# Sixteen experts on one core: the last six token tiles behind a branch on a count made on chip

## The chip, the cores and the metric

The kernel runs on one core of one Trainium2 chip. The metric is device time in microseconds of that core for one execution of the whole kernel. The kernel before takes 2091.18 us, the median of three runs (2089.25 to 2093.39).

## The reference, cut to what matters

Two layers of "graph attention, then feed-forward" over 3327 nodes with 256 features. The change lies in the first layer's feed-forward part, a mixture of 16 experts with the two best experts per token:

```python
logits = jnp.einsum('bsd,de->bse', x, gate_w) + gate_b
probs = jax.nn.softmax(logits, axis=-1)
top_probs, top_idx = jax.lax.top_k(probs, 2)
top_probs = top_probs / jnp.sum(top_probs, axis=-1, keepdims=True)
dispatch = jnp.sum(jax.nn.one_hot(top_idx, n_experts, dtype=x.dtype) * top_probs[..., None], axis=-2)
h1 = jnp.einsum('bsd,edh->bseh', x, w1)
h2 = jnp.einsum('bsd,edh->bseh', x, w2)
hidden = jax.nn.silu(h1) * h2
expert_out = jnp.einsum('bseh,eho->bseo', hidden, w3)
return jnp.einsum('bseo,bse->bso', expert_out, dispatch)
```

Here x is the layer-normalised node feature (256), the hidden width is 512, and only the two chosen experts of a token have a nonzero weight. Ahead of it stands a graph attention with two heads and a residual add; behind it a graph attention with one head, and a recurrence of 30 steps (tanh, silu, layer norm, a 256 x 256 product). All of that is the same in both kernels.

## The kernel before, in words

The nodes lie in 26 tiles of 128 rows. During the first graph attention every finished group of tiles is routed: normalised rows are written to a DRAM table (`table_x`), the gate picks two experts per token, and POOL's indirect DMAs write each token's number and weight into one list per expert (`lists`, line 551).

Only tokens that chose an expert are computed for it. Each expert's list is cut into tiles of 128 tokens, the last one partly empty. Whatever the routing, 2 x 3327 pairs over 16 experts fill at most `SLOTS` = (6654 - 16) // 128 + 16 = 67 tiles, and the kernel before works off 67 tiles always. Lines 605 to 675 make on chip, from the experts' counts (`cnt`: column 0 the tokens, column 2 the tiles, columns 3 and 4 the first tile and the end), the tables by tile: the expert (`table`, row 0), whether its weights differ from those three tiles earlier (`table`, row 1), which rows to gather (`which`), where to put results (`to`) and their weights. Tiles past the last expert's carry no tokens: `mine` is zero for them, their expert is 0, and their results go to spare rows of `given` that nothing reads.

The stage at lines 724 to 761 is a loop over tiles written out, on all engines at once. For each tile: POOL gathers 128 rows by indirect DMA four tiles ahead (line 685); TensorE transposes them (line 711) and ScalarE copies the result; TensorE multiplies with w1 (`pa`) and w2 (`pb`, both line 720); ScalarE takes silu of `pa` (line 741), VectorE multiplies with `pb` into `hidT` (line 744). One tile later TensorE multiplies `hidT` with w3 (`po`, line 751), VectorE scales by the token's weight (`y`, line 753), and POOL scatters `y` into the DRAM tensor `given` (line 754). Weights rotate through `SETS` = 3 sets of buffers; SyncE loads a set two tiles ahead (`weights`, lines 692 to 705), three DMAs of 512 KB, each carried out only when the register `new` is not zero. The first three sets are loaded unconditionally. SyncE reads expert and `new` from `table` into registers by one table load per tile.

After the stage, `add_results` (lines 776 to 785) reads `given` back by DMAs on SyncE (`th`, `z`, line 782), and VectorE or POOL adds them into x; then layer 1 begins with its projection. A scheduler puts the instructions in order within each engine and inserts the semaphore waits. The first reload of `given` waits for all scatters.

Of the kernel before, what the change touches and what calls it, by code (L numbers as in the profile page):

```python
# [10 lines left out]
F32 = mybir.dt.float32  # L11
I32 = mybir.dt.int32
BF16 = mybir.dt.bfloat16
FP8 = mybir.dt.float8e4
AF = mybir.ActivationFunctionType
ALU = mybir.AluOpType
# [3 lines left out]
P = 128  # L20
# [9 lines left out]
def gat_moe_gat_recurrent_ffn(ctx: ExitStack, tc: tile.TileContext, a: dict, out: bass.AP):  # L30
    nc = tc.nc
    N, D = a["x"].shape
# [6 lines left out]
    E = a["gate_w"].shape[1]  # L39
    HID = a["w1"].shape[2]  # L40
    FH = HID // P
# [255 lines left out]

    CAP = NT * P
    SLOTS = (2 * N - E) // P + E
    dram = ctx.enter_context(tc.tile_pool(name="dram", bufs=1, space=bass.MemoryType.DRAM))  # L300
    lists = dram.tile([E * CAP, 2], F32, name="lists")
    table_x = dram.tile([NP, D], F32, name="table_x")

    given = dram.tile([2 * NP + SLOTS * P, D], F32, name="given")
    in_bytes = dram.tile([MOST * P, NP], FP8, name="in_bytes")
# [24 lines left out]
    def score_vectors():  # L330

        for k in range(KD):
            for s in range(2):
                tc.keep_in_program_order(
                    nc.vector.scalar_tensor_tensor(
                        prod, wv1[:, k, :D], 1.0, va[:, s, :], op0=ALU.mult, op1=ALU.mult,
                        accum_out=wv1[:, k, D + s : D + s + 1],
                    )
                )

    with ExitStack() as moe:
        route_p = moe.enter_context(tc.tile_pool(name="route", bufs=1))
        ones = route_p.tile([P, P], F32, name="ones")
# [14 lines left out]
        with ExitStack() as st:  # L358
# [6 lines left out]
            ps_o = st.enter_context(tc.tile_pool(name="ps0o", bufs=2, space=PSUM))  # L365
# [5 lines left out]
            with ExitStack() as pre:  # L371
                work = pre.enter_context(tc.tile_pool(name="work0", bufs=2))
                hold = pre.enter_context(tc.tile_pool(name="hold0", bufs=1))
# [23 lines left out]
                for q, (s, h, k) in enumerate((s, h, k) for s in range(2) for h in range(H) for k in range(KD)):  # L397
                    nc.tensor.matmul(
                        pv[:, q : q + 1], lhsT=(w1, w2)[s][:, h, k * P : (k + 1) * P], rhs=aT[:, s, h : h + 1],
                        start=True, stop=True,  # L400
# [7 lines left out]
                for h in range(H):  # L408
                    for s, b in ((0, b1), (1, b2)):
                        nc.tensor.matmul(  # L410
                            pv[:, h : h + 1], lhsT=b[:, h : h + 1].to_broadcast([P, P]), rhs=aT[:, s, h : h + 1],
                            start=(s == 0), stop=(s == 1),
# [16 lines left out]
                behind = None  # L429
# [9 lines left out]
                for ts in groups0[1:3]:  # L439
                    behind = take_graph(ts, None, behind)  # L440
# [13 lines left out]
                for k in range(2):  # L454
                    numbers(pair[:, :, k, 0], [[P, NT]], k * NP, 1)
                nc.gpsimd.affine_select(
                    out=before, in_=ones, pattern=[[1, P]], compare_op=ALU.is_gt, fill=0.0, base=0, channel_multiplier=-1
# [13 lines left out]
            def route(ts):  # L471
# [103 lines left out]
        layer1_parameters()  # L575
        hold = moe.enter_context(tc.tile_pool(name="hold1", bufs=1))
        table = hold.tile([1, 2, SLOTS], I32, name="table")
        which = hold.tile([P, SLOTS], I32, name="which")
        to = hold.tile([P, SLOTS], I32, name="to")
        weight = hold.tile([P, SLOTS], F32, name="weight")  # L580
        SETS = 3
        ew = [
            (
                hold.tile([P, KD, HID], F32, name=f"ew1_{b}"),
                hold.tile([P, KD, HID], F32, name=f"ew2_{b}"),
                hold.tile([P, FH, D], F32, name=f"ew3_{b}"),
            )
            for b in range(SETS)
        ]
        with ExitStack() as pre:  # L590
# [5 lines left out]
            listed = ghold.tile([BLOCK, BLOCKS, P, 2], F32, name="listed")  # L596
            tile_no = ghold.tile([P, SLOTS], F32, name="tile_no")
            numbers(tile_no, [[1, SLOTS]], 0, 0)
# [3 lines left out]
            pc = ps_c.tile([P, 4], F32, name="pc")  # L602
            cnt = ghold.tile([E, 8], F32, name="cnt")
# [7 lines left out]
            nc.tensor.matmul(pc[:E, 1:2], lhsT=before[:E, :E], rhs=cnt[:, 2:3], start=True, stop=True)  # L611
            nc.vector.tensor_copy(cnt[:, 3:4], pc[:E, 1:2])
            nc.vector.tensor_tensor(cnt[:, 4:5], cnt[:, 3:4], cnt[:, 2:3], ALU.add)
            mine = ghold.tile([E, 2, SLOTS], F32, name="mine")
            nc.vector.tensor_scalar(mine[:, 0, :], tile_no[:E], cnt[:, 4:5], None, op0=ALU.is_ge)
            nc.vector.scalar_tensor_tensor(
# [61 lines left out]
        work = moe.enter_context(tc.tile_pool(name="work1", bufs=3))  # L678
        ps_t = moe.enter_context(tc.tile_pool(name="ps1t", bufs=1, space=PSUM))
        ps_h = moe.enter_context(tc.tile_pool(name="ps1h", bufs=2, space=PSUM))  # L680
        ps_o = moe.enter_context(tc.tile_pool(name="ps1o", bufs=2, space=PSUM))

        def gathered(s):
            row = rows_p.tile([P, D], F32, name="rows")
            nc.gpsimd.indirect_dma_start(  # L685
                out=row, out_offset=None, in_=table_x,
                in_offset=bass.IndirectOffsetOnAxis(ap=which[:, s : s + 1], axis=0),
            )
            return row

        behind = None

        def weights(s):
            nonlocal behind

            with tc.issue_after(behind) if behind else ExitStack():
                e, new = nc.values_load_multi_w_load_instructions(
                    table[0:1, 0:2, s], engines=[mybir.EngineType.SP], min_val=0, max_val=E - 1,
                    skip_runtime_bounds_check_because="numbers of experts, and 0 or 1",
                )[1]  # L700
            kw = {} if s < SETS else {"cond": new}
            w1, w2, w3 = ew[s % SETS]
            nc.sync.dma_start(w1, a["w1"][bass.ds(e, 1)].rearrange("e (k p) h -> p (e k) h", p=P), **kw)
            nc.sync.dma_start(w2, a["w2"][bass.ds(e, 1)].rearrange("e (k p) h -> p (e k) h", p=P), **kw)
            behind = nc.sync.dma_start(w3, a["w3"][bass.ds(e, 1)].rearrange("e (f p) o -> p (e f) o", p=P), **kw).ins

        def features_first(row):
            pt = ps_t.tile([P, KD, P], F32, name="pt")
            hT = work.tile([P, KD, P], F32, name="hT")
            for k in range(KD):  # L710
                nc.tensor.transpose(pt[:, k, :], row[:, k * P : (k + 1) * P], ident)  # L711
            nc.scalar.copy(hT, pt)  # L712
            return hT

        def product(hT, w, name):

            p = ps_h.tile([P, FH, P], F32, name=name)
            for f in range(FH):
                for k in range(KD):
                    nc.tensor.matmul(  # L720
                        p[:, f, :], lhsT=w[:, k, f * P : (f + 1) * P], rhs=hT[:, k, :],
                        start=(k == 0), stop=(k == KD - 1),
                    )
            return p


        ahead = [gathered(s) for s in range(min(4, SLOTS))]
        for s in range(SETS - 1):
            weights(s)
        hT = features_first(ahead.pop(0))  # L730
        made = None
        for s in range(SLOTS + 1):
            if s == 4:
                score_vectors()
            hidT = made
            if s < SLOTS:
                if s + 4 < SLOTS:
                    ahead.append(gathered(s + 4))
                pa = product(hT, ew[s % SETS][0], "pa")
                act = work.tile([P, FH, P], F32, name="act")  # L740
                nc.scalar.activation(act, pa, AF.Silu)  # L741
                pb = product(hT, ew[s % SETS][1], "pb")
                made = work.tile([P, FH, P], F32, name="hidT")
                nc.vector.tensor_tensor(made, act, pb, ALU.mult)  # L744
                if s + 1 < SLOTS:
                    hT = features_first(ahead.pop(0))
            if s > 0:
                w3 = ew[(s - 1) % SETS][2]
                po = ps_o.tile([P, D], F32, name="po")
                for f in range(FH):  # L750
                    nc.tensor.matmul(po, lhsT=hidT[:, f, :], rhs=w3[:, f, :], start=(f == 0), stop=(f == FH - 1))  # L751
                y = work.tile([P, D], F32, name="y")
                nc.vector.tensor_scalar(y, po, weight[:, s - 1 : s], None, op0=ALU.mult)
                put = nc.gpsimd.indirect_dma_start(
                    out=given, out_offset=bass.IndirectOffsetOnAxis(ap=to[:, s - 1 : s], axis=0), in_=y,
                    in_offset=None,
                )
                tc.declare_no_dep(put.ins, group="given", reason="no two results have the same row")
                tc.add_to_no_dep_group("given", put.ins)
            if s + SETS - 1 < SLOTS:  # L760
                weights(s + SETS - 1)

# [3 lines left out]
    with ExitStack() as st:  # L768
# [4 lines left out]
        work = st.enter_context(tc.tile_pool(name="work2", bufs=2))  # L773
        ps = st.enter_context(tc.tile_pool(name="ps2", bufs=2, space=PSUM))
        ps_o = st.enter_context(tc.tile_pool(name="ps2o", bufs=2, space=PSUM))
# [57 lines left out]
        pb = ps.tile([P, 512], F32, name="bank")[:, :D]  # L833
        for k in range(KD):
            nc.tensor.matmul(
                pb, lhsT=lb[:, k : k + 1].to_broadcast([P, P]), rhs=fW[:, k, :], start=(k == 0), stop=(k == KD - 1)
# [3 lines left out]
        pc = ps.tile([P, 512], F32, name="bank")[:, :D]  # L840
# [8 lines left out]
    with ExitStack() as st:  # L849
        ps_t = st.enter_context(tc.tile_pool(name="ps3t", bufs=2, space=PSUM))  # L850
        ps_o = st.enter_context(tc.tile_pool(name="ps3o", bufs=2, space=PSUM))
# [13 lines left out]
        for step in range(N_STEPS):  # L865
            for ts in groups:
# [17 lines left out]
                po = ps_o.tile([P, G, D], F32, name="po")  # L884
                for j in range(n):
                    for k in range(KD):
                        nc.tensor.matmul(  # L887
                            po[:, j, :], lhsT=zT[:, j, k, :], rhs=wc[:, k, :],
                            start=(k == 0), stop=(k == KD - 1),
# [62 lines left out]
```

## Time and profile before

| what | value |
|---|---|
| median of 3 runs | 2091.18 us |
| the profiled execution | 2091.22 us |
| its span, first to last instruction | 2089.5 us |
| TensorE busy in the span | 1974.8 us (95%) |
| experts' stage, 445.0 to 822.7 us | 377.7 us |
| matmuls `pa`, `pb` (16 records per tile each) | 275 ns each |
| matmuls `po` (8 records per tile) | 379 ns each |
| gathers and scatters on POOL | 67 each, 0.97 and 0.99 us median |
| weight DMAs issued by SyncE | 201, of 512 KB when carried out |
| mean granted TensorE clock | 0.979 of full speed |

Times are from the start of the span. Matmuls are pipelined, so records overlap: the distance between the starts of two tiles tells a tile's cost better than the sum of its records. A float32 product appears as two records per matmul of the program, each with a weight load. In the lists of instructions "SPq" is SyncE's queue; in the chain that ended last, every piece is what the next one waited for, and "issue" is time without a wait that the profile shows.

### The profile page before, as it was taken

The numbers are of one execution on the slowest core, as the hardware profiler recorded it, in microseconds if no ns is written. First come the engines' busy times: TensorE is split into PE (matmuls) and PEld (weight loads), VectorE is DVE, ScalarE is ACT, GpSimd is POOL, SyncE is SP. The second block draws the span as 40 slices with busy tenths as digits, with TensorE's granted clock in tenths as the row PEclk, the third lists the DMA queues.
The fourth block names the chain that finished last, engine by engine and source line by source line (L and its number), as shares of the span: only waits on it lengthen the run. The fifth ranks groups of instructions, "written<-read, shape, count | busy, mean of one in ns | idle before, by whom it ended". The sixth has DMA issues, their size and how long they took to land.

```text
span 2089.5 us, 34134 instructions
## 1 busy us (share of the span) xinstructions
PE 1974.8 (95%) x12252; PEld 1788.9 (86%) x12252; DVE 1304.8 (62%) x3824; ACT 1110.9 (53%) x1455; POOL 965.7 (46%) x896
## 2 busy tenths in 40 slices
PE   7999999749999997899999999999999999999998
PEld 6899999749999997688888888888888888888887
DVE  6787887712222222557766777777777777777777
ACT  2876766501111111656655666666566656665664
POOL 2010211343333332401100187777777777777775
PEclk9999999869999999899999999999999999999999
DMA  7878050067888883200000100000000000000003
GB/s 151 110 104 115 2 81 16 26 183 244 275 299 280 277 268 117 82 8 8 16 8 16 34 1 1 1 1 1 1 1 1 1 1 1 1 1 1 1 1 111
DMA packets 133438, 148.79 MB, mean 71 GB/s; under 512 B 51886, under 2 KB 95735, under 8 KB 133269
## 3 DMA queue, kind: packets, MB, share of 16 engines
q1 hardware_dynamic: 116577, 112.19, 17.9%
q0 software_dynamic: 12016, 29.66, 8.2%
q10 hardware_dynamic: 4676, 4.76, 0.8%
q8 instruction: 98, 1.61, 0.3%
q14 instruction: 71, 0.58, 0.1%
HBM read 174.37 MB, written 30.56 MB: 98 GB/s over the span
## 4 chain that ended last, share of the span: by engine, by line
PE 71%; ACT 5%; issue 1%; POOL 1%; DVE 1%; DMA 1%; SPq 0%; POOLq 0%; ACTq 0%; DVEq 0%
PE po L887 34%; PE acc L246 14%; PE pa L720 6%; PE pb L720 6%; PE po L751 6%; PE pt L881 4%; ACT zT L883 4%; PE pt L711 1%; PE acc L153 1%; POOL lists L551 0%; DMA z<-given 0%; PE bank L139 0%; POOL th L783 0%; DMA rows<-table_x,which 0%; POOL rstd L119 0%
## 5 line engine op out<-in xcount | busy, mean ns | idle before, releaser
L887 PE MATMUL po<-wc,zT 128*128 128x256 f32 x3120 | 705.5, 383 | 21.9 <-ACT zT L883 21.3
L887 PEld LDWEIGHTS po<-wc,zT 128*128 128x128 f32 x3120 | 582.9, 190 | 124.9 <-ACT zT L883 50.5
L246 PE MATMUL acc<-wh,pT 128*128 128x129 f32 (+1 forms) x4056 | 607.2, 311 | 7.0 <-DVE pT L241 6.7
L246 PEld LDWEIGHTS acc<-wh,pT 128*128 128x128 f32 x4056 | 563.7, 192 | 44.7 <-DVE pT L241 8.3
L236 ACT ACTIVATE e<-rb,minus,full 128x384 f32<-128x384 f32 (+3 forms) x494 | 401.3, 824 | 180.1 <-DVE pT L241 163.7
L873 POOL TENSOR_TENSOR th<-th,x 128x1024 f32<-128x1024 f32 (+1 forms) x210 | 461.2, 2214 | 63.7 <-ACT th L871 63.7
L241 DVE SCALAR_TENSOR_TENSOR pT<-e,part,adjT 128x384 f32<-128x384 f32 (+3 forms) x494 | 380.3, 773 | 146.3 <-PE acc L246 122.2
L892 DVE SCALAR_TENSOR_TENSOR x<-po,rr,bb 128x256 f32<-128x256 f32 x780 | 324.9, 477 | 118.2 <-PE po L887 113.4
L883 ACT COPY zT<-pt 128x1024 f32<-128x1024 f32 (+1 forms) x210 | 199.1, 948 | 332.7 <-PE pt L881 332.7
L879 DVE BATCH_NORM_STATS2 stats<-z 128x6 f32<-128x256 f32 x780 | 283.8, 415 | 117.5 <-ACT z L874 117.5
L119 POOL TENSOR_TENSOR rstd<-ve,neg_half 128x4 f32<-128x4 f32 (+3 forms) x28 | 31.2, 1116 | 408.0 <-DVE ve L117 312.4
L862 POOL TENSOR_TENSOR rr<-rr,neg_half 128x4 f32<-128x4 f32 (+1 forms) x210 | 207.5, 988 | 17.4
L874 ACT ACTIVATE z<-th 128x1024 f32<-128x1024 f32 (+1 forms) x210 | 210.6, 1003 | 0.9 <-POOL th L873 0.9
L871 ACT ACTIVATE th<-x 128x1024 f32<-128x1024 f32 (+1 forms) x210 | 199.3, 995 | 2.3 <-DVE x L128 1.4
L881 PE MATMUL pt<-ident,z 128*128 128x128 f32 x1560 | 189.9, 273 | 2.5 <-DVE high L817 2.5
L881 PEld LDWEIGHTS pt<-ident,z 128*128 128x128 f32 x1560 | 177.8, 141 | 14.8 <-issue 2.9
L744 DVE TENSOR_TENSOR hidT<-act,pb 128x512 f32<-128x512 f32 x67 | 46.1, 688 | 219.7 <-PE pb L720 216.2
L741 ACT ACTIVATE act<-pa 128x512 f32<-128x512 f32 x67 | 40.0, 597 | 205.1 <-PE pa L720 202.0
L720 PEld LDWEIGHTS pa<-hT,ew 128*128 128x128 f32 x1072 | 131.5, 194 | 5.0 <-ACT hT L712 1.7
L685 POOL DMA_INDIRECT rows<-table_x,which x67 | 64.6, 964 | 152.4 <-PE pt L711 136.8
L551 POOL DMA_INDIRECT lists<-pair,ati x52 | 60.2, 1157 | 160.8 <-DVE ati L538 85.2
L720 PE MATMUL pa<-hT,ew 128*128 128x128 f32 x1072 | 132.1, 277 | 1.0 <-ACT hT L712 1.0
(173 smaller groups left out, 1392.3 us busy)
## 6 DMA issues: line engine op xcount, KB each, us to landing
ew<-in_w_dram SPq DMA_DIRECT2D x201, 512.0 KB
in_bytes<-in_adj_dram POOLq DMA_DIRECT2D x3, 2496.0 KB, 28.2
x<-in_x_dram SPq DMA_DIRECT2D x6, 512.0 KB
th<-given SPq DMA_DIRECT2D x6, 512.0 KB
z<-given SPq DMA_DIRECT2D x6, 512.0 KB
kept<-x SPq DMA_DIRECT2D x8, 384.0 KB
old<-kept SPq DMA_DIRECT2D x6, 512.0 KB
out_dram<-x SPq DMA_DIRECT2D x6, 512.0 KB
```

What stands on the lines that cost most here:

```text
L236: nc.scalar.activation(e[:, : n * P], rb[:, : n * P], AF.Relu, scale=sc.full[:, j, h : h + 1], bias=sc.minus[:, j, h : h + 1],)
L241: masked = nc.vector.scalar_tensor_tensor(pT[:, : n * P], e[:, : n * P], sc.part[:, j, h : h + 1], adjT[:, j // 2, ts[0] * P : (ts[-1] + 1 ...
L246: nc.tensor.matmul(po[c], lhsT=pT[:, c * P : (c + 1) * P], rhs=wh[:, j, h, :], start=(j == 0 and c % per_bank == 0), stop=(j == NT - 1), s ...
L720: nc.tensor.matmul(p[:, f, :], lhsT=w[:, k, f * P : (f + 1) * P], rhs=hT[:, k, :], start=(k == 0), stop=(k == KD - 1),)
L862: nc.gpsimd.tensor_tensor(r[:, :n], r[:, :n], neg_half[:, :n], ALU.pow)
L873: nc.gpsimd.tensor_tensor(th[:, :n, :], th[:, :n, :], hs, ALU.add)
L874: nc.scalar.activation(z[:, :n, :], th[:, :n, :], AF.Silu, scale=1.0 / S)
L879: nc.vector.bn_stats(stats[:, j, :], z[:, j, :])
L881: nc.tensor.transpose(pt[:, j, k, :], z[:, j, k * P : (k + 1) * P], ident)
L883: nc.scalar.copy(zT[:, :n, :, :], pt[:, :n, :, :])
L887: nc.tensor.matmul(po[:, j, :], lhsT=zT[:, j, k, :], rhs=wc[:, k, :], start=(k == 0), stop=(k == KD - 1),)
L892: nc.vector.scalar_tensor_tensor(x[:, ts[0] + j, :], po[:, j, :], rr[:, j : j + 1], bb, op0=ALU.mult, op1=ALU.add)
```

## The change

The number of tiles that carry tokens is counted on chip: one matmul sums the tiles per expert (`cnt`, column 2) over the 16 experts, and a copy makes it an integer, `used`. The loop over tiles becomes a function `work_off(s0, s1)` over a stretch of tiles. `ALWAYS` is (2 x 3327 + 16 x 64) // 128 + 2 = 61. Tiles 0 to 60 are worked off as before. `used` is loaded into a register of every engine, and a block with tiles 61 to 66 runs only if it is above 61. The block is a pipeline of its own: it gathers and loads weights from its start, and drains before what follows. Its first three sets of weights (`fresh`) are loaded without a condition.

```diff
+    ALWAYS = (2 * N + E * P // 2) // P + 2
...
+        used = hold.tile([1, 1], I32, name="used")
...
+            nc.tensor.matmul(pc[0:1, 2:3], lhsT=cnt[:, 2:3], rhs=ones[:E, 0:1], start=True, stop=True)
+            nc.vector.tensor_copy(used, pc[0:1, 2:3])
...
-            kw = {} if s < SETS else {"cond": new}
+            kw = {} if s < SETS or s in fresh else {"cond": new}
...
-        ahead = [gathered(s) for s in range(min(4, SLOTS))]
-        for s in range(SETS - 1):
-            weights(s)
-        hT = features_first(ahead.pop(0))
-        made = None
-        for s in range(SLOTS + 1):
+        fresh = range(ALWAYS, ALWAYS + SETS)
+
+        def work_off(s0, s1):
+            ahead = [gathered(s) for s in range(s0, min(s0 + 4, s1))]
+            for s in range(s0, min(s0 + SETS - 1, s1)):
+                weights(s)
+            hT = features_first(ahead.pop(0))
+            made = None
+            for s in range(s0, s1 + 1):
...
+        loads, more = nc.values_load_multi_w_load_instructions(
+            used[0:1, 0:1], min_val=0, max_val=SLOTS, skip_runtime_bounds_check_because="a number of tiles"
+        )
+        for load in loads:
+            tc.keep_in_program_order(load)
+        work_off(0, ALWAYS)
+        behind = None
+        with tc.If(more[0] > ALWAYS):
+            work_off(ALWAYS, SLOTS)
```

The body of the loop is the same but for the bounds: `s < s1` for `s < SLOTS`, `s > s0` for `s > 0`, and so on. In the built program each engine loads the register and branches after its last instruction of tile 60. Where the block is skipped, an engine goes through a short arm in its place: it waits for its own earlier work and then raises its semaphores by as much as the block would have raised them, so that later waits hold in both cases; POOL does this for the eight semaphores of its DMAs, SyncE for those of its own. Then all engines continue with layer 1. Outside of the block the order of instructions on each engine is that of the kernel before, but for the two counting instructions.

More of the change, by code (lines that the diff above doesn't have):

```diff
@@ L724, in product @@
             return p
-        ahead = [gathered(s) for s in range(min(4, SLOTS))]
-        for s in range(SETS - 1):
-            weights(s)
-        hT = features_first(ahead.pop(0))
-        made = None
-        for s in range(SLOTS + 1):
[L733 to L761, printed above, removed]
@@ new lines, in gat_moe_gat_recurrent_ffn @@
+        fresh = range(ALWAYS, ALWAYS + SETS)
[6 more added lines that the diff above has]
+            for s in range(s0, s1 + 1):
+                if s == 4:
+                    score_vectors()
+                hidT = made
+                if s < s1:
+                    if s + 4 < s1:
+                        ahead.append(gathered(s + 4))
+                    pa = product(hT, ew[s % SETS][0], "pa")
+                    act = work.tile([P, FH, P], F32, name="act")
+                    nc.scalar.activation(act, pa, AF.Silu)
+                    pb = product(hT, ew[s % SETS][1], "pb")
+                    made = work.tile([P, FH, P], F32, name="hidT")
+                    nc.vector.tensor_tensor(made, act, pb, ALU.mult)
+                    if s + 1 < s1:
+                        hT = features_first(ahead.pop(0))
+                if s > s0:
+                    w3 = ew[(s - 1) % SETS][2]
+                    po = ps_o.tile([P, D], F32, name="po")
+                    for f in range(FH):
+                        nc.tensor.matmul(po, lhsT=hidT[:, f, :], rhs=w3[:, f, :], start=(f == 0), stop=(f == FH - 1))
+                    y = work.tile([P, D], F32, name="y")
+                    nc.vector.tensor_scalar(y, po, weight[:, s - 1 : s], None, op0=ALU.mult)
+                    put = nc.gpsimd.indirect_dma_start(
+                        out=given, out_offset=bass.IndirectOffsetOnAxis(ap=to[:, s - 1 : s], axis=0), in_=y,
+                        in_offset=None,
+                    )
+                    tc.declare_no_dep(put.ins, group="given", reason="no two results have the same row")
+                    tc.add_to_no_dep_group("given", put.ins)
+                if s + SETS - 1 < s1:
+                    weights(s + SETS - 1)
@@ L766, in gat_moe_gat_recurrent_ffn @@
+        loads, more = nc.values_load_multi_w_load_instructions(
+            used[0:1, 0:1], min_val=0, max_val=SLOTS, skip_runtime_bounds_check_because="a number of tiles"
+        )
+        for load in loads:
[4 more added lines that the diff above has]
+            work_off(ALWAYS, SLOTS)
     kept = dram.tile([NP, D], F32, name="kept")
```

## The prediction

> **What bounds the kernel now.** I read the windows by stage first, then the chain that ended last through the experts' stage, then SyncE's list of DMA issues near its end, and last the instruction queues. The windows say who is busy in the experts' stage and in the gap after it (columns: window, length, then busy us and instructions of PE, weight loads, DVE, ACT, POOL, then granted clock, DMA share, GB/s).
>
> ```profile
> 445.00:822.70 377.70, 372.15 (x2814) 357.36 (x2814) 79.67 (x142) 66.25 (x135) 129.45 (x133) 0.99 0.75 250
> 822.70:834.35 11.65, 0.00 (x0) 0.00 (x0) 3.07 (x9) 0.65 (x2) 2.12 (x5) 0.63 0.66 201
> ```
>
> TensorE is busy for 372.15 of 377.70 us, then for none of 11.65 us. The chain shows the pace and how the stage hands over (start us, us, what).
>
> ```profile
> 804.58 1.78 PE pa L720 x16
> ...
> 810.10 1.78 PE pa L720 x16
> ...
> 819.19 3.47 PE po L751 x16
> ...
> 822.68 0.50 DVE y L753
> ...
> 823.44 2.40 DMA given<-y,to
> 825.85 0.02 SPq L782
> 825.87 0.03 issue
> 825.90 0.03 SPq L782
> ...
> 827.47 6.71 DMA z<-given
> ```
>
> Two tiles' starts are 5.52 us apart; from 473.48 to 810.10 it is 336.62 / 61 = 5.518. A tile is 1.78 + 1.79 + 0.22 + 1.73 us of back-to-back PE work (pa, pb, transposes, po). The last tile then drains through DVE, POOL's scatter and its landing, three semaphore waits on SyncE (0.065 us each, waiting and gap), and the reload of `given`.
>
> The last view tells how many tiles carry tokens. A conditional weight load that is carried out occupies SyncE for about 0.37 us, a suppressed one for 0.08 us. These are the loads of w1 for tiles 59, 60, 62 and 63 (the 60th, 61st, 63rd and 64th of 67):
>
> ```profile
> 767.31 0.08 SPq L703 DMA_DIRECT2D ew<-in_w_dram  x1
> ...
> 772.52 0.38 SPq L703 DMA_DIRECT2D ew<-in_w_dram  x1
> ...
> 783.86 0.37 SPq L703 DMA_DIRECT2D ew<-in_w_dram  x1
> ...
> 789.41 0.08 SPq L703 DMA_DIRECT2D ew<-in_w_dram  x1
> ```
>
> A load is suppressed when the expert equals that of three tiles before. Over all 67 the pattern gives runs of 3, 5, 4, 3, 4, 4, 4, 3, 4, 3, 4, 4, 3, 4, 4, 4 tiles: sixteen experts and 60 tiles. Then come three loads (60 to 62) and four suppressed ones: the empty tiles, which fall back to expert 0. Routing worked through the reference's inputs gives the same sixteen numbers. So the count is 60, the limit `ALWAYS` is 61, and the block is jumped over.
>
> [...] No branch of this kind is in this trace, but its instruction queues can be read: 1.61 MB in 98 packets and 0.58 MB in 71, together 2.19 MB, which is 64 bytes for each of 34134 instructions. So a fetched piece is 16 KB on the large queue (about PE's share) and 8 KB on the other, 256 and 128 instructions. [...] granted 0.63 in the gap of 11.65 us. [...]
>
> **The change, part by part.**
>
> 1. Six tiles leave PE's path: 6 x 5.518 = 33.1 us. What else they did (six gathers, six scatters to spare rows, 18 weight issues of which the six of tiles 61 and 62 moved data, 12 ACT and 12 DVE operations) ran beside PE. Do those transfers set the pace rather than PE? No: tiles whose loads were suppressed (804.58 to 810.10) and tiles whose loads moved 1.5 MB (778.77 to 784.29, pb to pb) both take 5.52 us. The drain after the last tile is the same work in the same order, only after tile 60: last matmul 822.66, end of y 823.16, scatter issued 823.44 to 824.40, landed 825.85, first reload issued 826.03. I keep these times as coordinates for the costs below and take 33.1 off at the end.
>
> 2. Counting: one matmul with one output and one DVE copy to int32, near L611 to L613. Nearest rows: pc matmuls 0.21 us the pair, cnt copy 0.14 us, so up to 0.5 us with the waits. They stand at about 418 us in PE's and DVE's order; work there is covered by the listing scatters, the read of `listed` issued at 434.08 and the matmuls at 439.00, for which PE waited 18 us. The copy delays the `mine`, `pq`, `table` chain, so the first weight load (422.09) by up to 0.5 us; it is needed at 450.69. Cost 0; uncovered 0.5.
>
> 3. On each of the five engines: a load of the count into a register and a compare-and-branch, placed by the built order after the engine's last instruction of tile 60. The register load: in SyncE's list, issues at 799.09, 800.11 and 800.61 are 1.02 and 0.50 us apart, and only the first interval holds a table load, of two numbers: 0.52 us, an upper value for one number. [...] SyncE is done with its part long before (its last issue was at 810.13, 12 us ahead of PE's end), and ACT likewise. They wait in the empty arm at no cost.
>
> 4. The empty arm: each engine waits for its own earlier work, then raises its semaphores by what the skipped block would have raised. POOL waits for the scatters' landings and raises the eight scatter semaphores in one instruction. What follows (the reload of `given` on SyncE, `wh`'s memset on DVE) waits for all of these: a meeting of five engines. Queued behind SyncE's waits are all `th` and `z` reloads, and for those wait DVE, POOL and then all of layer 1.
>
> POOL, the last to arrive: scatter issued by 824.40, gap 0.30 as between its other DMA issues, load 0.52[...], still ahead of the landing at 825.85. From there five waits of 0.065 (0.33), then the raising instruction. The trace has none like it; POOL's shortest operations are 0.14 to 0.25 us and an indirect DMA 0.96, so 0.2 to 1.0. It ends at 826.4 to 827.2. SyncE then has twelve waits to run through, the first of which is on a POOL semaphore: 12 x 0.065 = 0.78. First reload at 827.2 to 828.0 instead of 826.03: 1.1 to 1.9 us later.
>
> 5. Instruction fetch at the branch. The block has 24 instructions on POOL, ACT and DVE and about 62 on SyncE, less than one 8 KB piece, so the target probably lies in what is already fetched; on PE it is 6 x 84 matmul and weight-load records, two 16 KB pieces, so PE probably fetches. A fetch from the trace: 0.3% of 16 engines' 2089.5 us over 98 packets is 1.0 us for a piece, plus at most the shortest landing of an indirect DMA, 2.4: from 0 (fetched ahead) to 3.4. [...] PE is needed again only at 834.35. So PE's fetch is hidden by POOL's path and the reload; if POOL too has to fetch, its arm starts at 828.7 and the first reload is at 830.0 to 830.8, 4.0 to 4.8 late.
>
> 6. What is late next: the reloads, DVE's add, POOL's add at 834.35, all by the same amount; after that everything keeps its order. New waits of a few times 0.065 us on ACT, POOL and PE in front of layer 1 fall into their idle time (ACT 15.67, PE 11.7 us). The unconditional loads of the first three tiles in the block are not carried out.
>
> Bounds of 3 to 6 together: 0 (POOL's instructions taken ahead) to 4.8. I take 2.0: the no-fetch sum of 1.1 to 1.9, plus a little for the chance of a fetch. Sum: -33.1 + 2.0 = -31.1. The profiled execution took 2091.22 (span 2089.5 and 1.7 around it), the median of the runs is 2091.18: no difference to carry over. 2091.2 - 31.1 = 2060.1 us.
>
> **Rivals.** *Fetches in series*: POOL or SyncE stalls at the branch and again at the jump out of the empty arm, 4.8 + 3.4 = 8.2 us, so 2066.3. For: two jumps on every engine. Against: short arms, and the code after the arm follows it directly. *Transfers set the pace*: then six mostly idle tiles would give back nothing like 33 us and the time would stay near 2091; the equal 5.52 us of loaded and unloaded tiles speaks against. *The block is entered*, the one on the slower side: from a count of 62 on, the pipeline starts anew after the branch. POOL issues the gather only at 825.3, row landing 4.45, transposes, copy and start 1.2: PE idles from 822.66 to about 831, 8.3 us, plus the meeting of 2: 2101.5. Count 60 in the trace speaks against; it would need a wrong number in the register.
>
> **How the numbers follow.** Skipped with the meeting at 0 to 4.8 us: 0.77. Fetches in series: 0.19. No gain to be seen: 0.01. Entered: 0.03. The likeliest case spans 2058.1 to 2062.9. With the runs' own spread (2089.25 to 2093.39) below, and the series of fetches above, the range is 2057.0 to 2066.5. About 0.2% (4 us) is what a measurement of this kernel can tell from no change, and both skipped cases gain over 24: faster 0.96, within 0.2% 0.01, slower 0.03.
>
> **What would show it.** Right: 61 tiles of pa, pb and po, w1 issues ending after the 61st, unchanged 5.52 us per tile, last po about 33 us earlier (789.6), first `th` reload some 5 us after it instead of 3.4, and from there the same lengths to the end. Step 4 or 5 is wrong if PE's gap of 11.65 us grows by much more or less than 2 us; the engine that enters the meeting last names the cause. Step 1 is wrong if the pace per tile changes. The prediction falls if 67 tiles appear.

## The result, and the profile after

The changed kernel takes 2059.79 us, the median of four runs (2058.68 to 2063.55), against 2090.22 us (2082.53 to 2093.39) for the kernel before, measured beside it. The ratio is 0.9863 with an interval of 0.9833 to 0.9893, a gain of 22 to 35 us. Forecast were 2060.1 us and a gain of 31.1. That the median lies only 0.3 us from the forecast is luck, as the four runs spread over 5 us.

| | before | after |
|---|---|---|
| the profiled execution | 2091.22 us | 2059.35 us |
| its span | 2089.5 us | 2057.6 us |
| tiles worked off | 67 | 61 |
| first `pa` matmul to last `po` matmul | 371.95 us | 338.81 us |
| end of the last `po` to first reload of `given` | 3.39 us | 5.66 us |
| start of the last scatter to first reload | 2.59 us | 4.87 us |

The windows of the kernel after, by stage (columns as for the kernel before: window, length, then busy us and instructions of PE, weight loads, DVE, ACT, POOL, then granted clock, DMA share, GB/s):

```profile
447.60:786.46 338.86, 338.35 (x2560) 325.25 (x2560) 72.62 (x129) 60.02 (x122) 112.76 (x117) 1.00 0.78 260
786.46:800.44 13.98, 0.00 (x0) 0.00 (x1) 3.09 (x9) 0.65 (x2) 2.15 (x5) 0.58 0.52 165
```

TensorE still sets the pace of the stage, now for 339 us. The gap in which it does nothing has grown from 11.7 to 13.98 us. In the chain that ended last, the tiles keep their distance, 779.43 less 773.91 or 5.52 us (the records overlap: a tile's 16 `pa` of 275 ns are 4.40 us in sum and a piece of 1.78):

```profile
773.91 1.78 PE pa L725 x16
...
779.43 1.78 PE pa L725 x16
...
783.00 3.47 PE po L759 x16
```

The hand-over behind the last tile, from the same view in a narrower window, shows the new piece: between the scatter's start and the first of SyncE's waits in the chain lie 4.12 us where there were 2.40, and SyncE then runs through a row of waits at 0.06 us each.

```profile
786.49 0.49 DVE y L761
...
787.25 4.12 DMA given<-y,to
...
791.39 0.02 SPq L800
791.41 0.04 issue
791.45 0.03 SPq L800
...
792.06 0.03 SPq L800
792.09 0.04 issue
792.12 0.38 SPq L800
```

What fills the 4.12 us is told by the view of the branch's line. Columns: line, engine's queue, operation, count, shortest, median and longest duration in ns, first and last start in us; what follows the semicolon can be passed over.

```profile
L778 POOLq EVENT_SEMAPHORE  x4: 17/43/43, 789.9 to 790.2; - x4
L778 SPq COMPARE_BRANCH  x1: 53/53/53, 774.7 to 774.7; - x1
...
L778 PEldq COMPARE_BRANCH  x1: 3889/3889/3889, 784.6 to 784.6; - x1
...
L778 POOLq COMPARE_BRANCH  x1: 45/45/45, 787.7 to 787.7; - x1
...
L778 PEldq EVENT_SEMAPHORE  x1: 51/51/51, 788.5 to 788.5; - x1
L778 POOLq INC_SWDGE_SEM  x1: 1187/1187/1187, 790.2 to 790.2; - x1
```

The scatter's landing is seen by POOL at 789.92, 2.67 us after its start. POOL's four waits take 0.33 us and the instruction that raises its eight DMA semaphores 1.19 us; then SyncE is let go. PE's branch took 3.89 us, but it began at 784.56, before PE's last matmuls were done, and PE was in its empty arm at 788.51, some 2.9 us ahead of POOL's end.

The difference of the two spans, 31.85 us, adds up from the two traces: the stage 33.14 less, the hand-over 2.27 more, first reload to POOL's first add 0.42 more (8.74 against 8.32), from there to the first matmul of the recurrence 1.62 more (355.64 against 354.02), the recurrence the same (901.13 in both); and the first `pa` stands 3.05 us earlier. The 0.42, the 1.62 and the 3.05 us can't be put down to the change: over the profiles of all kernels here, the first of these pieces lies between 8.2 and 9.3, the second between 353.4 and 358.1 and the first `pa` between 444.8 and 450.7, with and without a branch.

### The profile page after: what moved, and what is told of

It is laid out like the page before. It is cut to its first block, busy times and chain, and to the rows that moved or that the text cites. A ratio compares the mean times of both kernels' runs of the same rounds, so it can differ in the third digit from the quotient of the medians.

```text
span 2057.6 us, 33497 instructions
## 1 busy us (share of the span) xinstructions
PE 1940.5 (94%) x12002; PEld 1755.8 (85%) x12002; DVE 1298.3 (63%) x3813; ACT 1104.8 (54%) x1443; POOL 951.8 (46%) x884
## 4 chain that ended last, share of the span: by engine, by line
PE 70%; ACT 5%; issue 1%; DVE 1%; DMA 1%; POOL 1%; SPq 0%; POOLq 0%; DVEq 0%; ACTq 0%
PE po L905 34%; PE acc L246 14%; PE pa L725 5%; PE pb L725 5%; PE po L759 5%; PE pt L899 5%; ACT zT L901 4%; PE pt L716 1%; PE acc L153 1%; POOL lists L553 0%; DVE pT L241 0%; DMA z<-given 0%; PE bank L139 0%; POOL th L801 0%; DMA rows<-table_x,which 0%
## 5 line engine op out<-in xcount | busy, mean ns | idle before, releaser
L752 DVE TENSOR_TENSOR hidT<-act,pb 128x512 f32<-128x512 f32 x61 | 41.9, 688 | 200.9 <-PE pb L725 197.4
L725 PEld LDWEIGHTS pa<-hT,ew 128*128 128x128 f32 x976 | 119.8, 194 | 4.7 <-ACT hT L717 1.7
L690 POOL DMA_INDIRECT rows<-table_x,which x61 | 58.6, 961 | 138.5 <-PE pt L716 123.5
L725 PE MATMUL pa<-hT,ew 128*128 128x128 f32 x976 | 120.4, 277 | 1.0 <-ACT hT L717 1.0
```

Source lines behind the costliest of these rows:

```text
L725: nc.tensor.matmul(p[:, f, :], lhsT=w[:, k, f * P : (f + 1) * P], rhs=hT[:, k, :], start=(k == 0), stop=(k == KD - 1),)
```

## The experiments

The hand-over is measured below as "last scatter to first reload", in one trace per run. The "landing" is the moment at which the first engine that waits for the last scatter goes on. The runs e6, e7, e8, e10, e11 and e12 were made once each, for their traces; their total times are not used.

**e1: no branch, 61 tiles.** The output depends on the count being at most 61; the load of the count, the branch and the block are left out.

```diff
-        loads, more = nc.values_load_multi_w_load_instructions(
...
         work_off(0, ALWAYS)
-        behind = None
-        with tc.If(more[0] > ALWAYS):
-            work_off(ALWAYS, SLOTS)
```

> 61 tiles in one stretch, with no register load and no branch; tiles 61 to 66 are left out altogether. Theory (six tiles of PE work are 33.1 us, the branch costs 2.3 us at the hand-over): last scatter to first reload back to 2.6 us as in the kernel before (4.87 with the branch), total 33 us below the kernel before, about 2057.5, so 2.3 below the changed kernel. Rival (the branch is free, and the difference at the hand-over is given back later or is spread of the runs): total equal to the changed kernel's within 1 us, or the hand-over stays at 4.9 us.

Measured: 2060.15 us (2055.99 to 2062.38), ratio to the kernel before 0.9849 (0.9833 to 0.9866). The hand-over is back at 2.82 us, with the landing at 2.40 as in the kernel before:

```profile
788.98 2.40 DMA given<-y,to
791.38 0.02 SPq L792
...
791.80 0.37 SPq L792
```

So the branch's cost at the hand-over is shown, 2.05 us in this pair of traces. That the total gets 2.3 us better without it is not: it equals the changed kernel's, as the rival had it. Four runs that spread over 6 us don't resolve it, and in this trace the first tile took 7.39 us instead of 5.94.

**e2: all 67 tiles, and a block that can't be entered.**

```diff
-        work_off(0, ALWAYS)
+        work_off(0, SLOTS)
         behind = None
-        with tc.If(more[0] > ALWAYS):
+        with tc.If(more[0] > SLOTS):
```

> All 67 tiles always, and behind them the register loads, the branch and a block of six tiles that is never entered. Theory: the branch alone, last scatter to first reload 4.9 us instead of 2.6, total 2.3 us above the kernel before, some 2092.5. Rival (part of the gain of 31 us came from the branch or the new order of instructions, not from the tiles): total below the kernel before by more than its spread.

Measured: 2094.35 us, ratio 1.0020 (1.0010 to 1.0029), 2.1 to 6.1 us above the kernel before; the hand-over is 4.54 us. The trace holds no compare-and-branch: with a count of at most 67 the condition can never hold. So the branch was probably resolved in building; the empty arm alone is left, without the load of the count:

```profile
L778 POOLq EVENT_SEMAPHORE  x4: 17/42/43, 823.8 to 824.8; - x4
...
L778 POOLq INC_SWDGE_SEM  x1: 1427/1427/1427, 826.5 to 826.5; - x1
```

That sharpens the reading: of the 2.28 us that the hand-over lost in the changed kernel's trace, the arm alone accounts for 1.96, with no jump and no fetch of code. And no part of the gain comes from the branch.

**e3: the block entered.** All 67 tiles, the last six through the block.

```diff
-        with tc.If(more[0] > ALWAYS):
+        with tc.If(more[0] > 59):
```

> The changed kernel with the limit of the branch at 59 instead of 61, so that the block of six tiles is entered with the count of 60. Theory: all 67 tiles at 5.52 us, PE idle about 8 us at the branch while the block's first gather is issued, lands and is transposed: total 8 to 10 us above the kernel before, 2099 to 2102. Rival (the weights of tile 61 or the code of the block arrive later than the gathered rows): PE idle 12 us or more. Rival (the gathers run ahead of the branch): under 4 us.

Measured: 2105.05 us (2103.95 to 2107.64), ratio 1.0071 (1.0054 to 1.0088): 11.3 to 18.4 us above the kernel before, more than the 8 to 10 expected. TensorE's list at the branch:

```profile
787.80 0.81 PE L759 MATMUL po<-ew,hidT 128*128 128x256 f32 x3
797.42 0.66 PE L716 MATMUL pt<-ident,rows 128*128 128x128 f32 x2 [8.81 <-DMA rows<-table_x,which]
798.60 3.78 PE L725 MATMUL pa<-hT,ew 128*128 128x128 f32 x16 [0.52 <-ACT hT L717]
```

PE's last product ends at 788.61 and the block's first `pa` starts at 798.60: 10.0 us, not 8, but less than the 12 of the rival. The first gather was issued at 790.90, as early as expected, but landed after 6.5 us; five further gathers and the last tile's scatter stood in the same queue, and loads of weights of 512 KB each ran beside them; which of these delayed it isn't shown. And the first `pa` after PE's idle 8.81 us takes 3.78 us, where a set of 16 ahead of the branch takes 1.95 in the same trace (`pb` at 783.20). PE falls straight through its branch here, recorded with 0.09 us.

**e4: 60 tiles always.**

```diff
-    ALWAYS = (2 * N + E * P // 2) // P + 2
+    ALWAYS = (2 * N + E * P // 2) // P + 1
```

> 60 tiles always instead of 61, seven behind the branch, which is skipped at a count of 60. Theory: one tile of 5.52 us less on PE, nothing else: 5.5 us below the changed kernel, some 2054.3. Rival (a longer block costs more at the branch, or the stage's end is no longer set by PE): less than 4 us below it.

Measured: 2054.64 us (2051.87 to 2056.56), ratio 0.9825 (0.9808 to 0.9841), 5.15 us below the changed kernel's median: the fastest version of the study for this routing, though its interval overlaps the changed kernel's. But the hand-over in its trace is 6.17 us, 1.3 more than in the changed kernel's first trace, which was not expected. POOL waited for the landing until 4.2 us after the scatter's start:

```profile
L778 POOLq EVENT_SEMAPHORE  x4: 17/43/3459, 782.5 to 786.2; - x4
...
L778 PEldq COMPARE_BRANCH  x1: 3632/3632/3632, 779.2 to 779.2; - x1
...
L778 POOLq INC_SWDGE_SEM  x1: 1147/1147/1147, 786.2 to 786.2; - x1
```

**e5: 67 tiles, the last six without transfers.** They are neither gathered nor scattered and load no weights; PE, ACT and DVE work on what lies there. There is no branch.

```diff
-                        ahead.append(gathered(s + 4))
+                        ahead.append(gathered(s + 4) if s + 4 < ALWAYS else kept_row)
...
+                    if s > ALWAYS:
+                        continue
                     put = nc.gpsimd.indirect_dma_start(
...
-                if s + SETS - 1 < s1:
+                if s + SETS - 1 < ALWAYS:
```

> 67 tiles in one stretch without a branch, the last six of them without their gathers, scatters and weight loads: PE, ACT and DVE do their work on what the buffers hold. Theory (PE sets the pace): nothing gained but what the earlier last scatter gives at the hand-over, 0 to 3 us below the kernel before. Rival (the transfers of the six tiles were what the gain came from): 20 to 33 us below.

Measured: 2088.37 us, ratio 0.9985 (0.9973 to 0.9996), 0.8 to 5.6 us below the kernel before. The stage takes 373.25 us against 371.95; the difference of 1.3 is again the first tile. From the kernel before and from e5, first `pa` to last `po` (columns as above):

```profile
450.69:822.64 371.95, 371.49 (x2812) 357.08 (x2812) 79.65 (x141) 65.84 (x134) 124.94 (x129) 1.00 0.75 250
449.25:822.50 373.25, 372.78 (x2812) 358.37 (x2812) 79.67 (x141) 65.83 (x134) 114.11 (x117) 0.99 0.71 237
```

Only the hand-over is shorter, 0.59 us from the last `po` to the first reload against 3.39, as the last scatter had landed long before. So the transfers of the six tiles were worth nothing beyond the hand-over, and the gain of 33 us is PE's work.

**e6: a block fifteen times as long, never entered.**

```diff
         with tc.If(more[0] > ALWAYS):
-            work_off(ALWAYS, SLOTS)
+            for _ in range(15):
+                work_off(ALWAYS, SLOTS)
+                behind = None
```

> The changed kernel with a block fifteen times as long, still never entered: more than 360 instructions on POOL, ACT and DVE, over 900 on SyncE. Theory (a branch on POOL beyond the fetched code waits for it as PE's did, 3.9 us): POOL's compare-and-branch at least 2.5 us instead of 0.045, its arm entered 0.5 to 1.5 us after the scatter's landing, last scatter to first reload 5.4 to 6.4 us. Rival (the fetch is no matter of distance on these engines): 4.9 us as in the changed kernel.

Measured: hand-over 5.89 us, within what the theory expected, but not in the way it did. POOL's compare-and-branch is recorded with 53 ns; the time passes behind it. DVE's branch at 789.22 is followed by its arm only at 792.32, 3.0 us later, where the changed kernel has 0.5, and ACT's arm comes 2.5 us behind its branch instead of 0.1. Only the block's length differs, so distance matters on these engines too; that they waited for code is the likely reading.

```profile
L778 DVEq COMPARE_BRANCH  x1: 76/76/76, 789.2 to 789.2; - x1
...
L778 DVEq EVENT_SEMAPHORE  x1: 21/21/21, 792.3 to 792.3; - x1
```

On POOL a delay of that length would end at 792.7, and the scatter's landing was late as well (last packet at 792.41): which of the two held it can't be told from this run.

**e7: a block of one tile.** Tiles 62 to 66 are left out.

```diff
-            work_off(ALWAYS, SLOTS)
+            work_off(ALWAYS, ALWAYS + 1)
```

> The changed kernel with a block of one tile instead of six (tiles 62 to 66 left out), never entered. Theory (PE's 3.9 us at its branch is a fetch, and hidden by POOL's way): PE's branch under 0.5 us, last scatter to first reload unchanged at 4.9 us. Rival (PE's late arrival holds the meeting up): the hand-over falls by 1 us or more.

Measured: PE's branch 0.35 us, so its 3.9 us are a matter of distance. The hand-over from the scatter is 3.04 us, but this misleads: with one tile, POOL's arm waits for two semaphores only, neither of them the last scatter's, and its raising instruction ran at 787.18, ahead of the last scatter, whose own semaphore wait follows on POOL only at 788.40, and the scatter starts 1.7 us behind PE's end instead of 0.8. From PE's end to the first reload it is 4.72 us against 5.66. Neither theory had this; the run says nothing on who comes last.

**e8: a block without POOL's DMAs.** Its tiles are neither gathered nor scattered.

```diff
-            ahead = [gathered(s) for s in range(s0, min(s0 + 4, s1))]
+            ahead = [gathered(s) for s in range(s0, min(s0 + 4, s1))] if not s0 else [kept_row] * (s1 - s0)
...
-                    if s + 4 < s1:
+                    if s + 4 < s1 and not s0:
...
+                    if s0:
+                        if s + SETS - 1 < s1:
+                            weights(s + SETS - 1)
+                        continue
```

> The changed kernel with a block that issues no DMA on POOL (its six tiles are neither gathered nor scattered), never entered. Theory (the meeting costs POOL's four waits of 0.33 us and the raising instruction of 1.19 us, then SyncE's row of waits): the raising instruction is gone and last scatter to first reload falls by 1.2 to 1.5 us, to 3.3 to 3.7. Rival (the meeting as such costs, whoever comes last): 4.5 us or more.

Measured: the raising instruction is gone, but the hand-over only falls to 4.34 us: between the two expectations. Again the landing is late: SyncE's first wait passes 3.61 us after the scatter's start, against 2.40 in the kernel before.

**What the late landings have in common.** The trace times every DMA packet, those of code too. In e4, e6 and e8 nearly all of the scatter's packets end by 2.1 us, and a few (3 to 6) as late as 2.6 to 3.7. In the same time a second 16 KB packet of code runs on the queue that carries PE's code; the first one runs while PE is at its branch. Without a branch, before and in e1 and e2, no packet of code runs there and the last data packet ends at 2.05 to 2.06. Hence the last four runs.

**e9: as e4, with PE's part of the block cut to a quarter of the hidden width.** The block is not entered, so the output doesn't change.

```diff
-        def product(hT, w, name):
+        def product(hT, w, name, fs=FH):
...
-            for f in range(FH):
+            for f in range(fs):
...
-                    pa = product(hT, ew[s % SETS][0], "pa")
+                    pa = product(hT, ew[s % SETS][0], "pa", 1 if s0 else FH)
```

`pb` and `po` likewise.

> 60 tiles always as in e4, and a skipped block in which PE has only a quarter of the hidden width to do (the block's results would be wrong; it is not entered), so that PE's part is under 200 records instead of about 590. Theory (in e4 the hand-over of 6.2 us came from the fetch of code at PE's branch, whose second 16 KB piece ran on the DMA engines while the last scatter did and held some of its packets up by over a microsecond): PE's branch under 0.6 us, no code packet on PE's queue within the scatter, its last packet at 2.1 to 2.3 us instead of 3.7, last scatter to first reload 4.5 to 4.9 us. Total 1 to 1.5 us below e4, within the spread. Rival (a block of seven tiles costs more than one of six because more has to be raised or waited for): 5.8 us or more.

Measured: hand-over 4.84 us. PE's branch is short, no second packet of code runs beside the scatter, its last packet ends at 2.37 us, a little above what was expected.

```profile
L779 POOLq EVENT_SEMAPHORE  x4: 17/43/2130, 780.1 to 782.5; - x4
...
L779 PEldq COMPARE_BRANCH  x1: 352/352/352, 776.9 to 776.9; - x1
...
L779 POOLq INC_SWDGE_SEM  x1: 1147/1147/1147, 782.5 to 782.5; - x1
```

Total 2057.36 us (2051.30 to 2062.54), ratio 0.9859 (0.9841 to 0.9876): not below e4 but above it, with intervals that only just meet and runs that spread over 11 us. So the microsecond is seen in the trace alone.

**e10 and e11: the changed kernel and e4 once more, unaltered.**

> The changed kernel once more. Theory (the landing of the last scatter is late exactly where a fetched piece of code runs beside its packets): last scatter to first reload 4.8 to 5.0 us if PE's second piece starts after 2.1 us from the scatter, 5.3 to 6.3 us if it starts earlier. Rival (each kernel has its own fixed hand-over): 4.87 again whatever the fetch does.

> The kernel with 60 tiles always once more. Theory: as for the repeat of the changed kernel, 4.8 to 5.0 us if the second piece of code starts after the scatter's packets, 5.3 to 6.3 us if among them. Rival: 6.17 again whatever the fetch does.

Measured: 6.42 us and 5.84 us. The changed kernel has no fixed hand-over; the 4.87 us of its first trace was the good case. The expectation's dividing line was wrong, though: in e10 the second packet of code starts 2.12 us after the scatter, as late as in the first trace (2.07), and still the scatter's last packet, of 4 bytes, ends at 3.10 us and POOL sees the landing only at 4.22. In the first trace the last data packet ended at 2.17, while the code packet was already running. The chain of e10 shows the 5.67 us:

```profile
788.39 0.50 DVE y L761
...
789.16 5.67 DMA given<-y,to
```

**e12: e8 with PE's part cut as in e9.**

> The block of e8, without POOL's DMAs, and with PE's part cut to a quarter of the hidden width, never entered. Theory (what was left in e8 above its expectation was the late landing beside the fetch): no late packets, landing at 2.6 us with SyncE's row of twelve waits behind it, last scatter to first reload 3.2 to 3.5 us instead of 4.34. Rival (the meeting itself costs): 4.0 us or more.

Measured: hand-over 3.55 us, 0.05 above the range and far from the rival's 4.0: no second packet of code, last data packet at 2.33, SyncE's first wait passed at 2.82, and the rest is its row of waits. PE's branch here:

```profile
L786 PEldq COMPARE_BRANCH  x1: 350/350/350, 787.1 to 787.1; - x1
```

| kernel | second code packet, us from the last scatter | last data packet | landing seen | first reload |
|---|---|---|---|---|
| before | none | 2.06 | 2.40 | 2.59 |
| e1 | none | 2.05 | 2.40 | 2.82 |
| e2 | none | 2.05 | 2.42 | 4.54 |
| e12 | none | 2.33 | 2.82 | 3.55 |
| e9 | none | 2.37 | 2.87 | 4.84 |
| after | 2.07 to 3.06 | 2.17 | 2.67 | 4.87 |
| e10 | 2.12 to 3.09 | 3.10 | 4.22 | 6.42 |
| e11 | 1.75 to 2.75 | 3.38 | 3.87 | 5.84 |
| e4 | 1.68 to 3.00 | 3.70 | 4.20 | 6.17 |
| e6 | 1.57 to 2.58 | 3.21 | 3.69 | 5.89 |
| e8 | 1.42 to 2.51 | 3.12 | 3.61 | 4.34 |

Taking away the fetch (e4 to e9, e8 to e12) takes away 1.3 and 0.8 us. That the late data packets stood behind the code packet on one and the same DMA engine is the likely reading, and two things in the traces speak for it. In all five late traces a packet of the scatter starts within 0.02 us of the end of the 16 KB code packet. And in e4, e10 and e11 fifteen of the sixteen updates of the scatter's semaphore had come by 2.73 us, the last one at 3.84 to 4.19, as if one sixteenth of the transfer had been held up. It would also explain the first trace, where the code packet then ran on an engine that was done with its share. But the trace doesn't name the engine of a packet, so this last link is argued, not shown.

The traces from e12 down have also a code packet of 8 KB on the other code queue, within 1.1 to 2.0 us after the scatter (two in e6); before, e1 and e2 have none. It goes with the last data at 2.2 to 2.4 us instead of 2.05 in the three traces that are not late, and with a landing 0.3 to 0.5 us later.

## Why the prediction was right, point by point

- **Part 1, six tiles of PE work**: right. 33.14 us in the traces against 33.11, at an unchanged 5.52 us per tile; e5 shows that PE's work and not the transfers was the price. e4 fits the same price for a seventh tile (its median is 5.15 us lower, its pace 5.52), but the spread of the runs is as large.
- **The count from the suppressed loads**: right. 61 tiles ran, the block was skipped, and e3, which needs a count above 59, entered it.
- **Part 2, counting on chip, at 0**: not contradicted; first `pa` was not later (447.64 against 450.69), but its spread of 6 us over the profiles is far above the 0.5 at stake. No run priced it alone.
- **Part 3, load and branch**: the load took 0.30 to 0.62 us, near the 0.52 read from the trace. The branch took 0.05 to 0.08 us on all engines but PE; the small term for it in the prediction's times from 825.3 on was shown by no trace of before. Load and branch cost POOL nothing, since its sequencer had the load under way at 787.08, before the scatter began at 787.25.
- **Part 4, the meeting**: the mechanism was right in its order (POOL last, SyncE's row of waits behind it), the size a little low. Expected 1.1 to 1.9 us, measured 2.28. Two terms were short. The raising instruction took 1.19 us, where 0.2 to 1.0 had been taken. And POOL saw the landing 2.67 us after the scatter's start, where the 2.40 of before had been kept: 0.27 us more, with a code packet of 8 KB beside the scatter.
- **Part 5, the fetch at PE's branch**: that a branch past the code already fetched has to wait was the author's assumption, as no trace of before showed it; the runs speak for it, with 3.4 to 3.9 us on PE over six tiles or more and 0.35 over a short block. In the changed kernel PE's branch took 3.89 us, with a 16 KB code packet from 786.09 to 787.02 in it, against at most 3.4. The order of arrival, 822.66 + 0.52 + 3.4 = 826.6 us for PE and 826.4 to 827.2 for POOL by the prediction's terms, was borne out: POOL's path did hide PE's lateness, and e9 and e12 only gain what the landing gains. But the step was wrong in calling the fetch hidden, and so free. It runs on the DMA engines just when the last scatter has to land, and in five of six traces with a second packet of code the landing came 1.2 to 1.8 us later than the 2.4 before. The one without this is the trace of the result: here the prediction had luck. So the estimate of 2.0 for the meeting should have been 2.3 to 3.8 (hand-over 4.87 to 6.42), still within its stated bounds.
- **Part 6**: not contradicted. Behind the reload two pieces are 0.42 and 1.62 us longer and the rest is equal, and both differences lie within the spread over all traces. That a longer gap costs no longer slow start holds in this pair: from PE's first matmul behind the gap the granted clock was 0.50 for 5.12 us before (834.35 to 839.47) and for 5.20 us after (800.44 to 805.64), then 1.00 in both.
- **The rival on the slower side**: its direction and place were right, its size too small: 14.4 us above the kernel before (11.3 to 18.4) instead of 10. Two terms were short: the gather's landing (6.5 us, not 4.45) and the first `pa` behind the pause (3.78 us against 1.95, so 1.8 more), for which the prediction kept the full pace. One was too long: the meeting, taken at 2, cost 0.3 us, as last scatter to first reload was 2.89 us in e3; an entered block has no empty arm.

## What to carry to other kernels

Work that turns out empty is best priced on the engine that sets the pace: here a tile on TensorE, 5.5 us, not its transfers. A skipped block costs what its empty arm does to the path, not the jump (e2, without a jump, has 1.96 of the 2.28 us): count the waits for transfers in flight, the instructions that raise semaphores, and the row of waits behind them, and reckon with late data while code is fetched; here this was 2.3 to 3.8 us at a pipeline's drain; and an entered block costs a drained pipeline, here 14 us, so the limit belongs just above the usual count. A suppressed conditional DMA shows in the issue's duration (here about 0.08 us against 0.37), which lets a profile tell data-dependent counts without the data.

## What the runs showed of the hardware that was not expected

- PE's taken branch over the code of six tiles or more took 3.4 to 3.9 us in six traces, 0.35 us over a short block (e7, e9, e12), and 0.09 us where it fell through (e3).
- A fetch of code goes with late data: with a 16 KB code packet beside it, a 128-row scatter landed after 3.6 to 4.2 us in five of six traces; with an 8 KB packet alone after 2.8 to 2.9 us (e9, e12); without any after 2.4 us (before, e1, e2). Where only PE's part of the skipped block was cut, the 16 KB packet and the delay went away together.
- What a long block costs at a branch isn't always in the branch's record: DVE's compare-and-branch in e6 is recorded with 76 ns, and its next instruction comes 3.0 us later (0.5 in the changed kernel).
- The one instruction that raises POOL's eight DMA semaphores took 1.15 to 1.43 us. In e7, where POOL's arm waits for two semaphores only, it took 1.18.
